# Filling the block-diagonal weights of the product by C with transfers, and pairing places 64 apart

## The chip, the cores and the metric

The kernel runs on one core of a Trainium2 chip. The metric is the device time of one execution in microseconds (us). The core's engines are called PE (TensorE; PEld is its weight loads), DVE (VectorE), ACT (ScalarE), POOL (GpSimd) and SP (SyncE, which issues nearly all transfers here). SBUF is the on-chip memory of 128 partitions, PSUM the memory that PE writes, DRAM the large memory outside the core.

## What is computed

The reference is a network of four layers. Each layer normalizes x (64 images of 11 x 11 = 121 positions, 128 channels), passes it through a state-space mixer and adds the result, then passes it through a feed-forward part that differs from layer to layer and adds that. The change lies in the mixer, which is the same in all four layers and takes most of the time. Its core, cut to what matters:

```
xs    = silu(conv1d(x @ in_proj))             # 256 places l, 121 channels d
Bs,Cs = projections of xs                     # 16 states n, two directions k
delta = softplus(projection of xs)
dA    = exp(delta * A)                        # per channel, state and place
dBu   = delta * Bs * xs
h     = scan over l of  h = dA * h + dBu
y     = einsum('bkdln,bknl->bkdl', h, Cs) + Ds * xs
y     = y[:, 0] + flip(y[:, 1])               # second direction runs backwards
```

The last product, y = sum over the 16 states n of h times C, is the one that is changed. For every image b, place l and channel d it is a sum of 16 terms whose weights C depend on b, n and l.

## The kernel before, in words

**Tiling.** A mixer handles the 64 images in eight chunks c of eight images (CB = 8). The 128 partitions hold the pairs (state n, image b), partition 8n + b. For each chunk there are two *passes* m = 2c and 2c + 1, one for each direction k (odd m goes backwards over the places). A pass runs over 61 pairs of channels, one *step* each; its first step is s = 61 m. A layer so has 16 passes and 976 steps, the kernel 64 passes.

**One step.** PE expands delta to the 128 partitions (`rows`, L677, into one of five PSUM tiles da; three steps ahead of the scan), ACT takes its exponentials (`exps`, L690), and DVE scans two channels (`scan`, L698) with da and the tile ub as inputs, into a tile H. ub holds delta times x for four channels, loaded from DRAM 14 steps ahead (`load_u`, L654, seven buffers, 512 KB each) and multiplied by B on POOL five steps ahead (`times_b`, L666). H and HX, two tiles, take the scans of 16 steps in turn (the groups dq = 0 to 3 of a pass).

**The product by C.** When a group of 16 steps is scanned, PE forms its y during the next 16 steps (`by_c`, L719): 32 *slots*, each four matmuls that lie beside each other in PE's columns. Each matmul takes 16 weights per partition: two places times eight images, where the weights are zero unless the partition's image is the column's. So one matmul sums over the 16 states for eight images, and two places share it. The results gather in the PSUM tile yb (eight slots); after every eight slots `keep_y` (L734 and L736) copies yb to the SBUF tile yst (even m, on ACT) or adds it there (odd m, on DVE). After each odd pass yst is stored to DRAM by 16 transfers (`store_y`, L751, 60.5 KB each) at steps 8 to 11 and 16 to 19 of the next pass.

**The weights.** `load_bc` (L636) loads B and C of a pass as two tiles Bt and Cp of 128 x 256, 18 steps before the pass. `own_c` (L643) makes the block-diagonal weights on POOL: a product of Cp, broadcast over eight columns, with a constant mask `own`, 128 x 512 elements, into one of four tiles Cz. It runs four times in a pass, at steps 8, 12, 16 and 20; slots 8u to 8u + 7 read Cz[u]. The group dq = 0 starts its product at step 16 of the pass.

**What sets the order.** The order is written out by hand: `run` puts each piece of work under a step (`self.at(step, f)`), and for every step the program issues, in this order, what is under `pre` (keep_y), the rows and exponentials of the step three ahead, loads and products of ub, the scan, and the plan of that step. Each engine takes its instructions in that order, SP's transfers too. Waits are set where data or buffers need them. A transfer on SP also takes one of eight semaphores in turn, so that an issue waits for the landing of the transfer eight before it.

In the even passes from m = 2 on, SP's queue holds, besides ub: the stores of y, the loads of R (L627, the operand of `rows`; the third part of a pass is loaded at step 20), and the loads ts and y of the tail of the chunk before (L453 and L455, at step 22), which PE and DVE use at steps 31 and 32.

Of the kernel before, what the change touches and what calls it, by code (L numbers as in the profile page):

```python
# [8 lines left out]
F32 = mybir.dt.float32  # L9
# [3 lines left out]
AX = mybir.AxisListType  # L13
# [3 lines left out]
D = 121  # L17
C = 128
L = 256
NS = 16  # L20
# [57 lines left out]
CB = 8  # L78
# [8 lines left out]
class Conv:  # L87
# [38 lines left out]
    def made(self, setup, fixed, ps, in_x, conv_wT, x_dt, dt_wT):  # L126
        cx, nc, a = self.cx, self.nc, self.cx.a
        p = f"L{self.l}_conv_"
        af = self.A.rearrange("p k d -> p (k d)")
        nc.scalar.activation(af, af, AF.Exp)  # L130
        nc.vector.tensor_scalar_mul(af, af, -1.0)


        pick = setup.tile([5 * 24, 5, CB], F32, name="pick")
        nc.vector.reduce_sum(pick, cx.ident[:120, :120].rearrange("p (a s b) -> p a b s", s=3, b=CB), axis=AX.X)
        self.pick = fixed.tile([5 * 24, 5, NS, CB], BF16, name="pick16")
        for i in range(5):
# [24 lines left out]

    def buffers(self, fixed, work, ps_f, dram):
        cx, nc, NC = self.cx, self.nc, self.NC
        self.work = work

        self.H = [fixed.tile([128, 2 * L, 16], F32, name="H"), cx.HX.rearrange("p (a w) -> p a w", w=16)]
        self.spare = [x.rearrange("p a w -> p (a w)") for x in self.H]
        self.da = [ps_f.tile([128, 2, L], F32, name=f"da{i}") for i in range(RING)]
        self.yb = ps_f.tile([128, 8, 2, 2, 16], F32, name="yb")  # L170
        nc.vector.memset(self.yb, 0.0)
        self.Cz = [fixed.tile([128, 64, CB], F32, name=f"Cz{i}") for i in range(4)]
        self.t = fixed.tile([128, CB, L], F32, name="t")
# [454 lines left out]
        if q == 3:  # L628
            nc.sync.dma_start(R[:24, 3, :], rows[24 * 120 : 24 * 121])

    def load_bc(self, m):
        c, k = m // 2, m % 2
        for name, at in (("Bt", 0), ("Cp", NS)):
            x = self.work.tile([128, L], F32, name=name, bufs=2)
            r0 = 2 * NS * k + at
            self.nc.sync.dma_start(x, self.bcD[c, r0 : r0 + NS].rearrange("r b l -> (r b) l"))  # L636
            self.bc[m, name] = x

    def own_c(self, m, u):

        C = self.bc[m, "Cp"]
        C = C[:, L - 1 - 64 * u : (L - 65 - 64 * u if u < 3 else None) : -1] if m % 2 else C[:, 64 * u : 64 * u + 64]
        self.nc.gpsimd.tensor_mul(  # L643
            self.Cz[u],
            C.unsqueeze(2).to_broadcast([128, 64, CB]),
            self.own.unsqueeze(1).to_broadcast([128, 64, CB]),
        )

    def load_u(self, T):
        m, i = divmod(T, TILES)  # L650
# [11 lines left out]
    def times_b(self, T):  # L662
        m, i = divmod(T, TILES)
        n = min(4, D - 4 * i)
        x = self.ub[T][:, :n, :]
        self.nc.gpsimd.tensor_mul(x, x, self.bc[m, "Bt"].unsqueeze(1).to_broadcast([128, n, L]))  # L666

    def channels(self, p):
        return min(2, D - 2 * p)
# [37 lines left out]
    def by_c(self, m, dq, slot):  # L707


        w = DQ[dq][1]  # L710
        H = self.H[dq % 2].rearrange("p (j l) w -> p l j w", l=L)
        for q in range(4):
            place = 8 * slot + 2 * q
            if m % 2:
                l = L - 1 - place
                h = H[:, l : (l - 2 if l > 1 else None) : -1, :, :w]
            else:
                h = H[:, place : place + 2, :, :w]
            self.nc.tensor.matmul(  # L719
                self.yb[32 * q : 32 * q + 16, slot % 8, :, :, :w],  # L720
                self.Cz[slot // 8][:, place % 64 : place % 64 + 2, :].rearrange("p l b -> p (l b)"),
                h,
                start=True,
                stop=True,
                skip_group_check=True,
            )
# [16 lines left out]
        if dq == 3:  # L743
            put(y[:, :, D - 1 : D], yb[:, :, 0, n : n + 1])

    def store_y(self, m, half, q, j):
        out = self.yD[m // 2].rearrange("(s x) (b d) -> x b s d", x=8, d=D)
        y = self.yst.rearrange("p (s x) d -> p s x d", x=2)
        rows = slice(16 * half, 16 * half + 16)
        p = 32 * q + 8 * j  # L750
        self.nc.sync.dma_start(out[2 * q + j][:, rows, :], y[p : p + 8, rows, j, :])  # L751


    def at(self, step, *fs):
# [15 lines left out]

    def run(self):
        NC, G = self.NC, 2 * self.NC * PAIRS
        self.R, self.bc, self.ub, self.pre = {}, {}, {}, {}
        NT = 2 * NC * TILES
        first = [PAIRS * (T // TILES) + 2 * (T % TILES) for T in range(NT)]

# [9 lines left out]
        for c in range(NC):  # L786
            s = STEPS * c
# [686 lines left out]
```

## Time and profile before

| what | value |
|---|---|
| median of 3 runs | 8470.6 us (8464.77 to 8479.49) |
| span of the profiled execution | 8458.2 us, 209204 instructions |
| PE busy | 5994.4 us (71%) |
| DVE busy | 6141.0 us (73%) |
| ACT busy | 5768.7 us (68%) |
| POOL busy | 5832.5 us (69%) |
| SP's transfers | 1588.21 MB, 930871 packets, 74.6% of the 16 transfer engines' time |
| mean granted clock of PE | 0.78 of full speed |
| mixers (first to last scan of each layer) | 79.5 to 1724.2, 2089.2 to 3728.0, 4037.8 to 5680.3 and 5994.4 to 7623.3 us |

The profile is of one execution. A line of a group of instructions reads: line of the kernel, engine, operation, written tile <- read tiles, shape, count | busy time in us, mean ns of one | idle time of the engine before it, and what ended most of that. In the view of waits a line reads: who waited <- for whom: us in all, times, the longest. In the timeline: start and length in us, engine, line, operation, tiles, how many; in square brackets the idle time before it and what ended that; SPq is SP issuing transfers, and its length there includes waits. A busy engine is not at its peak, and idle time of an engine that nobody waits for costs nothing.

### The profile page before, as it was taken

Reading aid. Unit: us, or ns where it says so; the run is one execution under the profiler, and the core shown is the slowest. Engines: PE = TensorE matmul, PEld = TensorE weight load, DVE = VectorE, ACT = ScalarE, POOL = GpSimd, SP = SyncE. Lnnn points to the kernel's source line nnn. Section 1 sums busy time; section 2 is a strip of 40 time slices with the busy share of each in tenths; the row PEclk is TensorE's granted clock in tenths of the full one; section 3 lists DMA queues with packets and bytes.
Section 4 is the critical chain, followed back from the end, with each engine's and each line's share of the span. In section 5 each row is a group of like instructions: output and inputs, shape, how many; then the busy total and the mean of one; then the engine's idle time right before and its main releaser. Section 6 shows DMA issues by size and latency. Waiting matters only on the chain.

```text
span 8458.2 us, 209204 instructions
## 1 busy us (share of the span) xinstructions
PE 5994.4 (71%) x83374; PEld 3445.8 (41%) x83374; DVE 6141.0 (73%) x8636; ACT 5768.7 (68%) x12927; POOL 5832.5 (69%) x3139
## 2 busy tenths in 40 slices
PE   5676677676677767767677777666567776766999
PEld 3343343355344434344344444344333433433445
DVE  6888888854888888872788888882688888883211
ACT  6888888743888878862788788863688888873210
POOL 6888888921988888850888888870688888890000
PEclk7777777767777777776777777766777778778999
DMA  6888998946898899960899999981689888992111
GB/s 171 221 224 223 223 226 225 232 140 177 218 224 225 224 220 222 230 181 25 222 220 227 221 226 226 224 205 31 179 226 225 230 225 226 226 231 72 39 34 37
DMA packets 933130, 1603.70 MB, mean 190 GB/s; under 512 B 139912, under 2 KB 620514, under 8 KB 932151
## 3 DMA queue, kind: packets, MB, share of 16 engines
q1 hardware_dynamic: 930871, 1588.21, 74.6%
q8 instruction: 655, 10.73, 0.6%
q14 instruction: 324, 2.65, 0.1%
q10 hardware_dynamic: 1280, 2.10, 0.1%
HBM read 1299.53 MB, written 290.52 MB: 188 GB/s over the span
## 4 chain that ended last, share of the span: by engine, by line
PE 31%; ACT 20%; DMA 17%; DVE 14%; issue 8%; POOL 7%; SPq 1%; DVEq 0%; POOLq 0%; ACTq 0%
ACT da L690 7%; DVE H L698 5%; DMA ub<-uD 5%; POOL ub L666 5%; PE da L677 4%; PE yb L719 4%; PE pc L253 4%; DVE HX L698 3%; DMA ts<-sD 3%; PE pu L1306 3%; PE acc L1309 3%; PE out L1349 2%; DMA uD<-u 2%; PE pst L1193 2%; DMA R<-dD 2%
## 5 line engine op out<-in xcount | busy, mean ns | idle before, releaser
L666 POOL TENSOR_TENSOR ub<-ub,Bt 128x1024 f32<-128x1024 f32 (+1 forms) x1984 | 4564.0, 2317 | 731.8 <-DMA ub<-uD 526.1
L690 ACT ACTIVATE da<-da,A 128x255 f32<-128x255 f32 x7744 | 3389.6, 446 | 1094.7 <-PE da L677 918.7
L698 DVE TENSOR_TENSOR_SCAN H<-da,ub 128x512 f32<-128x512 f32 x2048 | 2391.8, 1205 | 93.6 <-POOL ub L666 42.0
L677 PE MATMUL da<-R,pick 120*128 120x255 bf16 x7744 | 1783.5, 324 | 938.0 <-DVE H L698 529.4
L698 DVE TENSOR_TENSOR_SCAN HX<-da,ub 128x512 f32<-128x512 f32 (+1 forms) x1856 | 2115.6, 1187 | 90.5 <-issue 52.4
L677 PEld LDWEIGHTS <-pick 120*128 120x128 bf16 x7744 | 599.6, 104 | 1638.3 <-issue 777.1
L719 PE MATMUL yb<-H,Cz 128*16 128x64 f32 x32768 | 867.6, 255 | 349.8 <-ACT yst L736 260.4
L719 PE MATMUL yb<-HX,Cz 128*16 128x64 f32 x32768 | 856.5, 246 | 209.9 <-ACT yst L736 102.5
L719 PEld LDWEIGHTS yb<-H,Cz 128*16 128x16 f32 x32768 | 604.5, 112 | 921.4 <-issue 520.1
L719 PEld LDWEIGHTS yb<-HX,Cz 128*16 128x16 f32 x32768 | 562.4, 110 | 680.7 <-issue 316.8
L734 DVE TENSOR_TENSOR yst<-yst,yb 128x512 f32<-128x512 f32 (+2 forms) x640 | 340.2, 548 | 272.7 <-PE yb L719 272.5
L253 PE MATMUL pc<-w_conv,xnT 128*121 128x256 f32 x1344 | 441.6, 426 | 55.2 <-ACT t L257 55.1
L174 POOL MEMSET t<- 128x2048 f32 x4 | 7.2, 1804 | 597.4 <-PE px L1200 416.3
L736 ACT COPY yst<-yb 128x512 f32<-128x512 f32 (+2 forms) x640 | 330.6, 543 | 109.3 <-DMA yD<-yst 43.1
L304 PE MATMUL pd<-t,w_dt 122*128 122x512 f32 x480 | 358.3, 839 | 54.6 <-ACT t L264 54.6
L339 POOL TENSOR_TENSOR u<-relu,t 128x512 f32<-128x512 f32 x240 | 307.2, 1280 | 22.7 <-DVE relu L330 22.6
L350 POOL TENSOR_TENSOR d<-relu,d 128x512 bf16<-128x512 f32 x240 | 278.6, 1161 | 54.1 <-ACT d L346 53.9
L1273 DVE COPY U<-pu 128x488 f32<-128x488 f32 x128 | 85.4, 667 | 283.4 <-PE pu L1306 283.4
L1275 ACT COPY U<-pu 128x488 f32<-128x488 f32 x128 | 72.9, 569 | 309.2 <-PE pu L1306 309.2
L343 POOL TENSOR_TENSOR relu<-relu,d 128x512 f32<-128x512 f32 x240 | 279.1, 1163 | 6.6
L253 PEld LDWEIGHTS pc<-w_conv,xnT 128*121 128x121 f32 x1344 | 233.7, 209 | 102.8 <-ACT t L257 81.6
L643 POOL TENSOR_TENSOR Cz<-Cp,own 128x512 f32<-128x512 f32 x256 | 274.4, 1072 | 0.0
(242 smaller groups left out, 7929.8 us busy)
## 6 DMA issues: line engine op xcount, KB each, us to landing
ub<-uD SPq DMA_DIRECT2D x1920, 512.0 KB
dD<-d SPq DMA_DIRECT2D x256, 384.0 KB
R<-dD SPq DMA_DIRECT2D x192, 420.0 KB
uD<-u SPq DMA_DIRECT2D x256, 256.0 KB
sD<-s SPq DMA_DIRECT2D x128, 256.0 KB
yD<-yst SPq DMA_DIRECT2D x512, 60.5 KB
ts<-sD SPq DMA_DIRECT2D x56, 512.0 KB
y<-yD SPq DMA_DIRECT2D x112, 242.0 KB
```

Source lines behind the costliest of these rows:

```text
L253: nc.tensor.matmul(pc, lhs, rhs, start=(j == 0), stop=(j == taps - 1))
L304: nc.tensor.matmul(s["p"], self.w_dt[:, k, :], tb[: D + 1], start=True, stop=True)
L339: nc.gpsimd.tensor_mul(s["u"], s["relu"], tb)
L343: less.tensor_sub(s["relu"], s["relu"], s["d"][:, 0, :])
L350: less.tensor_sub(s["d"][:, 2, :], s["relu"], s["d"][:, 1, :])
L666: self.nc.gpsimd.tensor_mul(x, x, self.bc[m, "Bt"].unsqueeze(1).to_broadcast([128, n, L]))
L677: self.nc.tensor.matmul(self.da[g % RING][:, j, 1:], self.pick[:n, d % 5].rearrange("p n b -> p (n b)"), self.R[m, d // 35][:n, d % 35 // ...
L690: self.nc.scalar.activation(x, x, AF.Exp, scale=self.A[:, m % 2, d : d + 1])
L698: self.nc.vector.tensor_tensor_scan(self.H[dq % 2][:, :n, p - DQ[dq][0]], self.da[g % RING].rearrange("p j l -> p (j l)")[:, :n], x.rearra ...
L719: self.nc.tensor.matmul(self.yb[32 * q : 32 * q + 16, slot % 8, :, :, :w], self.Cz[slot // 8][:, place % 64 : place % 64 + 2, :].rearrange ...
L734: nc.vector.tensor_add(dst, dst, src)
L736: nc.scalar.copy(dst, src)
```

## The change

The tiles Cz become two, each laid out as two blocks x of 64 places by eight images, [128, x, b, 64], and both are cleared on POOL once per layer. `own_c`, its mask and the load of Cp go. Instead `load_c` fills, for each pass, each tile and each image b, the 16 partitions 8n + b of the image's own block from DRAM: 16 transfers per pass (two tiles, eight images), each of 16 x 2 x 64 elements, 8 KB. They stand at steps 9 and 10 (first tile) and 17 and 18 (second tile), four to a step. What lies outside an image's own block stays zero for the whole layer.

A matmul now takes the places l and l + 64 of one tile: its 16 weights stand 64 elements apart, and its moving rows are two places 64 apart. Slots 0 to 15 read the first tile, 16 to 31 the second. Since another place comes out where, `store_y` writes other rows of DRAM, in as many transfers of the same size.

```diff
-        self.own = fixed.tile([128, CB], F32, name="own")
-        nc.vector.reduce_sum(self.own, cx.ident.rearrange("p (n b) -> p b n", b=CB), axis=AX.X)
...
-        self.Cz = [fixed.tile([128, 64, CB], F32, name=f"Cz{i}") for i in range(4)]
+        self.Cz = [fixed.tile([128, 2, CB, 64], F32, name=f"Cz{i}") for i in range(2)]
+        for x in self.Cz:
+            nc.gpsimd.memset(x, 0.0)
...
-    def own_c(self, m, u):
-
-        C = self.bc[m, "Cp"]
-        C = C[:, L - 1 - 64 * u : (L - 65 - 64 * u if u < 3 else None) : -1] if m % 2 else C[:, 64 * u : 64 * u + 64]
-        self.nc.gpsimd.tensor_mul(
-            self.Cz[u],
-            C.unsqueeze(2).to_broadcast([128, 64, CB]),
-            self.own.unsqueeze(1).to_broadcast([128, 64, CB]),
-        )
+    def load_c(self, m, u, b):
+
+        rows = self.bcD[m // 2, 2 * NS * (m % 2) + NS : 2 * NS * (m % 2) + 2 * NS, b, :]
+        blocks = rows.rearrange("r (x l) -> r x l", l=64)
+        blocks = blocks[:, (1 - u) * 2 + 1 : (1 - u) * 2 - 1 if u == 0 else None : -1] if m % 2 else blocks[:, 2 * u : 2 * u + 2]
+        self.nc.sync.dma_start(self.Cz[u][b : b + 121 : CB, :, b], blocks)
...
+        C = self.Cz[slot // 16].rearrange("p x b l -> p (x b l)")
         for q in range(4):
-            place = 8 * slot + 2 * q
+            at = 4 * (slot % 16) + q
+            place = 128 * (slot // 16) + at
             if m % 2:
-                l = L - 1 - place
-                h = H[:, l : (l - 2 if l > 1 else None) : -1, :, :w]
+                l, at = L - 1 - place, 63 - at
+                h = H[:, l : (l - 65 if l > 64 else None) : -64, :, :w]
             else:
-                h = H[:, place : place + 2, :, :w]
+                h = H[:, place : place + 65 : 64, :, :w]
...
-                self.Cz[slot // 8][:, place % 64 : place % 64 + 2, :].rearrange("p l b -> p (l b)"),
+                C[:, at::64],
...
-    def store_y(self, m, half, q, j):
-        out = self.yD[m // 2].rearrange("(s x) (b d) -> x b s d", x=8, d=D)
+    def store_y(self, m, half, q, x):
+        out = self.yD[m // 2].rearrange("(h x s q) (b d) -> h x q b s d", h=2, x=2, q=4, d=D)
...
-            self.at(max(s - 18, 0), lambda m=m: self.load_bc(m))
-            for u in range(4):
-                self.at(s + 8 + 4 * u, lambda m=m, u=u: self.own_c(m, u))
+            self.at(max(s - 18, 0), lambda m=m: self.load_b(m))
+            for u in range(2):
+                for b in range(CB):
+                    self.at(s + 9 + 8 * u + b // 4, lambda m=m, u=u, b=b: self.load_c(m, u, b))
```

More of the change, by code (lines that the diff above doesn't have):

```diff
@@ L629, in load_r, with load_b @@
             nc.sync.dma_start(R[:24, 3, :], rows[24 * 120 : 24 * 121])
[L631 to L637, printed above, removed]
-    def own_c(self, m, u):
-        C = self.bc[m, "Cp"]
-        C = C[:, L - 1 - 64 * u : (L - 65 - 64 * u if u < 3 else None) : -1] if m % 2 else C[:, 64 * u : 64 * u + 64]
-        self.nc.gpsimd.tensor_mul(
-            self.Cz[u],
-            C.unsqueeze(2).to_broadcast([128, 64, CB]),
-            self.own.unsqueeze(1).to_broadcast([128, 64, CB]),
-        )
+    def load_b(self, m):
+        c, r0 = m // 2, 2 * NS * (m % 2)
+        x = self.work.tile([128, L], F32, name="Bt", bufs=2)
+        self.nc.sync.dma_start(x, self.bcD[c, r0 : r0 + NS].rearrange("r b l -> (r b) l"))
+        self.B[m] = x
+    def load_c(self, m, u, b):
[3 more added lines that the diff above has]
+        self.nc.sync.dma_start(self.Cz[u][b : b + 121 : CB, :, b], blocks)
     def load_u(self, T):
@@ L665, in times_b @@
         x = self.ub[T][:, :n, :]
-        self.nc.gpsimd.tensor_mul(x, x, self.bc[m, "Bt"].unsqueeze(1).to_broadcast([128, n, L]))
+        self.nc.gpsimd.tensor_mul(x, x, self.B[m].unsqueeze(1).to_broadcast([128, n, L]))
     def channels(self, p):
@@ L744, in keep_y @@
             put(y[:, :, D - 1 : D], yb[:, :, 0, n : n + 1])
-    def store_y(self, m, half, q, j):
-        out = self.yD[m // 2].rearrange("(s x) (b d) -> x b s d", x=8, d=D)
+    def store_y(self, m, half, q, x):
+        out = self.yD[m // 2].rearrange("(h x s q) (b d) -> h x q b s d", h=2, x=2, q=4, d=D)
         y = self.yst.rearrange("p (s x) d -> p s x d", x=2)
-        rows = slice(16 * half, 16 * half + 16)
-        p = 32 * q + 8 * j
-        self.nc.sync.dma_start(out[2 * q + j][:, rows, :], y[p : p + 8, rows, j, :])
+        self.nc.sync.dma_start(
+            out[half, x, q], y[32 * q + 8 * x : 32 * q + 8 * x + 8, 16 * half : 16 * half + 16, x, :]
+        )
     def at(self, step, *fs):
@@ L772, in run @@
         NC, G = self.NC, 2 * self.NC * PAIRS
-        self.R, self.bc, self.ub, self.pre = {}, {}, {}, {}
+        self.R, self.B, self.ub, self.pre = {}, {}, {}, {}
         NT = 2 * NC * TILES
```

## The prediction

> **What bounds the kernel now.** I read the page first, its busy times and its costliest groups, for what the change takes away:
>
> ```profile
> PE 5994.4 (71%) x83374; PEld 3445.8 (41%) x83374; DVE 6141.0 (73%) x8636; ACT 5768.7 (68%) x12927; POOL 5832.5 (69%) x3139
> ...
> L643 POOL TENSOR_TENSOR Cz<-Cp,own 128x512 f32<-128x512 f32 x256 | 274.4, 1072 | 0.0
> ```
>
> POOL (GpSimd) carries 5832.5 us, nearly as much as DVE, and L643, which goes, is 274.4 us of it: 256 products of 1.07 us, four in each of the 64 passes. Whether those are worth anything depends on who waits for POOL, so the view of waits is next:
>
> ```profile
> POOL ub L666 <- DMA ub<-uD: 526.1, 402, 13.4
> ...
> DVE yst L734 <- PE yb L719: 272.5, 175, 4.8
> ...
> DVE y L468 <- DMA y<-yD: 90.5, 23, 8.2
> ...
> DVE H L698 <- POOL ub L666: 42.0, 11, 12.8
> ...
> DVE HX L698 <- POOL ub L666: 9.5, 8, 3.1
> ```
>
> The reader is to see two things. POOL's longest wait is for a transfer, and the scans (L698), which pace a pass, wait for POOL only 42.0 + 9.5 us. DVE waits more for the product by C (PE, L719) and for loads. The view of the tile Cp shows the product once more, and below it (the line of PE's weight loads) who waited for it, us and times:
>
> ```profile
> L643 POOL TENSOR_TENSOR Cz<-Cp,own x256: 1055/1070/1122, 94.8 to 7570.7; 128x512 f32<-128x512 f32 x128
> ...
>   PEld yb L719: 38.7, 25
> ```
>
> So PE's weight loads waited 38.7 us for it in all.
>
> From the scans' starts in the trace (passes 2 to 14 of each layer) a pass of even m takes about 109 us and one of odd m about 99, and two scans of one unbroken run start 1.11 us apart. Even passes hold the loads of the next eight images, the tail of the last eight and, from m = 2 on, the 16 stores of y (L751), which stand in SP's queue among the loads of ub. The timeline of SP, and then of DVE, in one such pass (layer 0, m = 6; its step 17 ends at 740.7 us, its step 24 starts at 747.3 us):
>
> ```profile
> 741.03 0.51 SPq L654 DMA_DIRECT2D ub<-uD  x1
> 741.60 2.82 SPq L751 DMA_DIRECT2D yD<-yst  x4
> 744.55 0.64 SPq L654 DMA_DIRECT2D ub<-uD  x1
> 745.30 0.62 SPq L353 DMA_DIRECT2D dD<-d  x1
> 745.96 1.66 SPq L354 DMA_DIRECT2D uD<-u  x1
> 747.98 2.34 SPq L751 DMA_DIRECT2D yD<-yst  x4
> 750.42 0.65 SPq L654 DMA_DIRECT2D ub<-uD  x1
> ...
> 753.58 0.43 SPq L453 DMA_DIRECT2D ts<-sD  x1
> ```
>
> ```profile
> 738.66 15.91 DVE L698 TENSOR_TENSOR_SCAN HX<-da,ub 128x512 f32<-128x512 f32 x14
> ```
>
> From 741.60 to 750.42 SP issues 11 transfers in 8.82 us, 0.80 us each, without a pause: here **SP is full**, because the program gives SP's transfers eight semaphores in turn and an issue waits until the eighth one before it has landed. By the landing events in the trace a store of y takes 5.8 us from issue to landing (median; a tenth of them under 3.5), a load of ub 6.9. DVE meanwhile runs 14 scans without a gap, so nothing there can be late for free.
>
> **The change part by part.**
>
> *Removed on POOL.* 256 x 1.072 = 274 us. What it is worth is what others wait for: at most 42.0 + 9.5 + 38.7 = 90 us, at least nothing; I take 28, since most of those waits stand elsewhere in the passes. The 64 loads of Cp go too (SP, issued 18 steps ahead, 0.4 us each): 0.
>
> *Added on POOL and PE.* Two clearings per layer at its start; L174's row prices 128x2048 at 1804 ns, so an estimate of 0.9 us each, 7 us in all, beside 80 us before the first scan: 0. The first product on each new tile waits for up to seven semaphores; such a wait on PE's sequencer takes 51 ns by the trace, 128 x 6 x 51 ns = 39 us at most; it lies within the wait for the data: 0.
>
> *Moved on PE.* As many matmuls and weight loads, but the 16 weights of a partition lie 256 B apart and the moving rows in four runs of 64 B. Passes of odd m read such runs today (their places go backwards): their matmuls have 254 ns against 247 in even passes, so the runs cost nothing. No row has strided weights. Bounds: nothing, or as if all columns between were loaded, 209 ns (L253's load of 121 columns) instead of 97 to 112; nearest is the scan L698, which writes every sixteenth element and keeps its 1.11 us, so 0.
>
> *Stores of y.* As many, of the same size, other rows: 0.
>
> *Added on the transfer engines.* 4 x 16 x 16 = 1024 transfers of 32 pieces of 256 B. By the trace's packets a piece of 484 B takes 31 ns (median) and one of 1 KB 46: 32,768 x 31 ns / 16 = 63 us, less 64 x 128 x 46 ns / 16 = 24 us for Cp: +40 us of mean share over some 6,600 us, and the shares (0.86 to 0.93 in such stretches) have that room: 0.
>
> *Added in SP's queue, and on the path.* 16 more issues in each pass, at steps 9, 10, 17 and 18, behind a load of ub that waits for the scan of its own step. Behind them stand the next loads of ub, in even passes the stores of y, the load of R (step 20) and the tail's ts and y (step 22); and the product of slot 0 (slot 16) now waits for eight of them to land. By the trace, slot 0 starts 12.9 us after the end of scan 9 in even passes and 10.1 in odd ones; slot 16 starts 8.3 us after the end of scan 17 in even ones and 11.4 in odd ones. That is the time SP has.
>
> Even passes with stores (7 x 4 = 28): from the first store of the second burst, the last load of Cz1 is the 15th issue (4 stores, 4 loads, ub, 2 stores, 4 loads). At 0.7 us an issue (below the 0.80 above, as the new transfers are smaller) it goes out 14 x 0.7 = 9.8 us after 741.6 and lands 5 us later (between 3.5 and 5.8): 756.4, with 0.5 left over from the first burst 757. The product of slot 16 started at 749.9: it is 7 us late. PE takes its instructions in the program's order, so the rows of step 28 (L677) and their exponentials are late behind it, and DVE has at most a step in hand: **6 us per pass**, 168 us. The tail says the same: 16 x 0.7 = 11.2 us more for SP before ts and y, less 4.4 us that SP idles between the two bursts today, so they go out 6.8 us later; DVE waits for them now at step 32 (5.2 us per even pass). Both delays are one shift of the pass, so the larger is counted, not the sum.
>
> Odd passes (32): the loads of step 10 wait for the ub load of step 8 (8.2 us) eight places before; the last is issued some 9 us after scan 9 and lands at 11 to 13, against 10.1: 1 to 2.5 us late, of which PE and DVE have about one in hand: 1 us, 32 us. Their loads of ub have 10 us in hand there (4 on landing, 6 after POOL): 0. The 4 first passes, without stores: 2 us each, 8 us.
>
> Sum: 168 + 32 + 8 - 28 = **+180 us**. The profiled execution's span is 8458.2; the median of the runs is 8470.6, 12.4 more, which lies around the span and stays. 8470.6 + 180 = **8650 us**.
>
> Ends. Low: 0.45 us an issue and 3.5 to land puts slot 16 only 1.5 us late, 0.5 x 28 = 14, odd passes nothing, POOL worth 90: 8395. High: 0.84 us an issue (the mean of the second bursts) and 5.8 to land: 759.2, with 1.2 left over 10.5 late, 9.5 x 28 + 2.5 x 32 + 4 x 4 = 362: 8833.
>
> The Trainium skill ("DMA: Bandwidth & Descriptors", Rules for kernel authors) speaks against this change: many small transfers are to be made one, and under 64 KB one pays mostly overhead; these are 8 KB. Its Anatomy of one DMA puts the fixed part at about 2 us, where the trace has 5.8 us for stores of 60 KB behind full queues; with 2 us to land, slot 16 would be 4 us late and the sum an estimate of 8570. The measured landing decides.
>
> **The rivals.**
>
> *It is faster.* The small transfers go out at the fastest issue of a store, 0.35 us, and land in 3 us: 14 x 0.35 + 3 = 7.9 us, inside the 8.3 us that slot 16 leaves. Then nothing new is late and POOL's relief stands, up to 90 us: 8380 to 8450, say 8430. For it: SP is idle for two thirds of a pass. Against it: the 11 issues in 8.82 us. It decides at 8.3 us from scan 17 to the landing of Cz1.
>
> *Hidden anyway.* Half of the lateness is absorbed, and POOL's relief pays the rest: within 17 us of 8470.
>
> *Much slower.* SP's lag reaches the loads of R and ub in odd passes too (11 us per pass x 64 = 700), or strided weights load slowly: 8850 to 9200.
>
> **How the numbers follow.** The forecast's case (slower by 20 to 360 us) 0.60, faster 0.21, hidden 0.07, much slower 0.12. The range that takes in the ends is 8400 to 8830. About 0.2%, 17 us, is what a measurement of this kernel can tell from no change: faster 0.21, same 0.07, slower 0.72.
>
> **What would show it.** Right: in the view of waits, PE (yb, L715 then) waiting for transfers of Cz, mostly at step 24 of even passes; SP's timeline there without pauses, the tail's ts and y 5 to 8 us later after the first store; even passes 5 to 8 us longer, odd ones 0 to 2; POOL 274 us less busy and waiting longer for ub. Wrong: no such wait and shorter passes (faster), or weight loads over 112 ns (strided weights).

## The result and the profile after

The changed kernel takes 8891.2 us (median of 4 runs, 8871.1 to 8901.4); the kernel before took 8467.7 us in the runs beside it. The ratio is 1.050, with a 95% interval of 1.0481 to 1.0515: 423 us slower, where the forecast had 180 and a range that ended at 8830. The profiled execution's span is 8883.8 us against 8458.2. Below, "us slower" is always the difference of the medians of runs on one chip.

From the page of the changed kernel: the busy times, and the groups that answer to what the prediction priced (the product by B, and the scans into the tiles H and HX).

```profile
PE 6249.4 (70%) x83374; PEld 3701.2 (42%) x83374; DVE 6269.0 (71%) x8632; ACT 5876.7 (66%) x12927; POOL 5913.0 (67%) x2891
...
L660 POOL TENSOR_TENSOR ub<-ub,Bt 128x1024 f32<-128x1024 f32 (+1 forms) x1984 | 4836.1, 2466 | 1016.7 <-DMA ub<-uD 807.3
...
L692 DVE TENSOR_TENSOR_SCAN H<-da,ub 128x512 f32<-128x512 f32 x2048 | 2444.6, 1241 | 121.5 <-POOL ub L660 60.5
...
L692 DVE TENSOR_TENSOR_SCAN HX<-da,ub 128x512 f32<-128x512 f32 (+1 forms) x1856 | 2157.2, 1213 | 340.6 <-issue 233.8
```

POOL lost 256 products of 1.07 us, and is yet 80 us busier than before. The count of its instructions fell from 3139 to 2891; what rose is the mean of the product by B, from 2317 to 2466 ns (1984 of them: +296 us). The scans rose from 1205 and 1187 to 1241 and 1213 ns, in a line that the change does not touch. The same three groups on the page of the kernel before:

```profile
L666 POOL TENSOR_TENSOR ub<-ub,Bt 128x1024 f32<-128x1024 f32 (+1 forms) x1984 | 4564.0, 2317 | 731.8 <-DMA ub<-uD 526.1
...
L698 DVE TENSOR_TENSOR_SCAN H<-da,ub 128x512 f32<-128x512 f32 x2048 | 2391.8, 1205 | 93.6 <-POOL ub L666 42.0
...
L698 DVE TENSOR_TENSOR_SCAN HX<-da,ub 128x512 f32<-128x512 f32 (+1 forms) x1856 | 2115.6, 1187 | 90.5 <-issue 52.4
```

Something makes instructions longer on engines that do what they did before. It is not PE's granted clock, which is lower here (mean 0.764 for 0.778): in before_dummy below it is lower still, 0.758, and the three durations are 2316, 1207 and 1188 ns.

The view of waits of the changed kernel (who <- for whom: us in all, times, longest):

```profile
PE yb L715 <- DMA Cz<-bcD: 349.3, 66, 13.3
DVE yst L730 <- PE yb L715: 331.7, 210, 4.7
...
DVE y L467 <- DMA y<-yD: 59.7, 20, 6.3
```

The new wait stands there: PE's product by C waits 349.3 us for transfers into Cz, up to 13.3 us at a time. The scans' new gap (233.8 us on the page of the changed kernel, 52.4 before) is put down to "issue", which means that the view found no releaser; the timelines show which it is. First the view of the tile Cz, after and before (least, median and longest ns; then first and last start):

```profile
L715 PEld LDWEIGHTS yb<-H,Cz x32768: 104/146/196, 106.2 to 8045.0; 128*16 128x16 f32 x200
```

```profile
L719 PEld LDWEIGHTS yb<-H,Cz x32768: 92/97/151, 106.7 to 7619.8; 128*16 128x16 f32 x200
```

A weight load takes 146 ns at the median. Before it took 97.

Now the same even pass that the prediction showed (layer 0, m = 6), in the timeline of SP after the change, from the second half of the stores of y on. Step 17's scan ends at 773.2 us.

```profile
773.84 3.18 SPq L745 DMA_DIRECT2D yD<-yst  x4
777.12 6.30 SPq L641 DMA_DIRECT2D Cz<-bcD  x4
783.53 0.53 SPq L648 DMA_DIRECT2D ub<-uD  x1
784.15 0.55 SPq L352 DMA_DIRECT2D dD<-d  x1
784.76 0.62 SPq L353 DMA_DIRECT2D uD<-u  x1
785.42 2.08 SPq L745 DMA_DIRECT2D yD<-yst  x2
787.55 3.37 SPq L641 DMA_DIRECT2D Cz<-bcD  x4
790.97 0.84 SPq L745 DMA_DIRECT2D yD<-yst  x2
...
794.36 0.64 SPq L452 DMA_DIRECT2D ts<-sD  x1
```

The issue of the last transfer into the second tile, the 17th from the first store on, ends at 790.9, 17.1 us after that store began. Then PE's timeline over the same time:

```profile
792.38 0.87 PE L715 MATMUL yb<-H,Cz 128*16 128x64 f32 x24 [9.57 <-DMA Cz<-bcD]
793.18 0.61 PE L671 MATMUL da<-R,pick 120*128 120x255 bf16 x2
```

and DVE's:

```profile
770.85 11.51 DVE L692 TENSOR_TENSOR_SCAN HX<-da,ub 128x512 f32<-128x512 f32 x10
782.86 2.34 DVE L692 TENSOR_TENSOR_SCAN HX<-da,ub 128x512 f32<-128x512 f32 x2 [0.50 <-issue]
794.84 1.23 DVE L692 TENSOR_TENSOR_SCAN HX<-da,ub 128x512 f32<-128x512 f32 x1 [9.64 <-issue]
```

Read the three together: PE stands 9.57 us in front of slot 16; behind that product in PE's order are the rows of step 28 (L671, 793.18), then their exponentials on ACT, then the scan, which comes after 9.64 us without work. This chain is the one that the prediction described, and it is longer.

By the scans' starts (means of passes 2 to 14 of each layer), an even pass went from 107.4 to 117.5 us and an odd one from 99.5 to 103.6. Of the even ones' 10.1 us, 8.4 arise at the scan after step 27. The odd passes' 4.1 us are spread over many steps, none of which adds more than 0.9. So there are two losses of different shape: one gap in even passes, and something thin everywhere.

### The profile page after: what moved, and what is told of

It is laid out like the page before. It is cut to its first block, busy times and chain, and to the rows that moved or that the text cites. A ratio compares the mean times of both kernels' runs of the same rounds, so it can differ in the third digit from the quotient of the medians.

```text
span 8883.8 us, 210188 instructions
## 1 busy us (share of the span) xinstructions
PE 6249.4 (70%) x83374; PEld 3701.2 (42%) x83374; DVE 6269.0 (71%) x8632; ACT 5876.7 (66%) x12927; POOL 5913.0 (67%) x2891
## 4 chain that ended last, share of the span: by engine, by line
PE 31%; ACT 19%; DMA 18%; DVE 14%; issue 8%; POOL 6%; SPq 4%; DVEq 0%; POOLq 0%; ACTq 0%
DMA ub<-uD 8%; ACT da L684 6%; DVE H L692 6%; PE yb L715 5%; POOL ub L660 5%; PE da L671 4%; PE pc L252 3%; DMA ts<-sD 2%; PE pu L1303 2%; PE acc L1306 2%; DVE HX L692 2%; PE out L1346 2%; SPq L641 2%; PE pst L1190 2%; DMA bcD<-bc 2%
## 5 line engine op out<-in xcount | busy, mean ns | idle before, releaser
L660 POOL TENSOR_TENSOR ub<-ub,Bt 128x1024 f32<-128x1024 f32 (+1 forms) x1984 | 4836.1, 2466 | 1016.7 <-DMA ub<-uD 807.3
L692 DVE TENSOR_TENSOR_SCAN H<-da,ub 128x512 f32<-128x512 f32 x2048 | 2444.6, 1241 | 121.5 <-POOL ub L660 60.5
L671 PE MATMUL da<-R,pick 120*128 120x255 bf16 x7744 | 1795.5, 327 | 864.5 <-DVE H L692 509.3
L692 DVE TENSOR_TENSOR_SCAN HX<-da,ub 128x512 f32<-128x512 f32 (+1 forms) x1856 | 2157.2, 1213 | 340.6 <-issue 233.8
L715 PE MATMUL yb<-H,Cz 128*16 128x64 f32 x32768 | 956.6, 265 | 645.2 <-DMA Cz<-bcD 349.3
L671 PEld LDWEIGHTS <-pick 120*128 120x128 bf16 x7744 | 599.0, 105 | 1535.9 <-issue 748.2
L715 PEld LDWEIGHTS yb<-H,Cz 128*16 128x16 f32 x32768 | 706.3, 144 | 1243.6 <-issue 722.7
L715 PE MATMUL yb<-HX,Cz 128*16 128x64 f32 x32768 | 948.5, 256 | 187.1 <-ACT yst L732 91.9
L715 PEld LDWEIGHTS yb<-HX,Cz 128*16 128x16 f32 x32768 | 681.3, 146 | 651.7 <-issue 308.1
L349 POOL TENSOR_TENSOR d<-relu,d 128x512 bf16<-128x512 f32 x240 | 291.1, 1213 | 117.1 <-ACT d L345 114.8
L338 POOL TENSOR_TENSOR u<-relu,t 128x512 f32<-128x512 f32 x240 | 336.8, 1403 | 19.1 <-ACT da L684 18.5
L342 POOL TENSOR_TENSOR relu<-relu,d 128x512 f32<-128x512 f32 x240 | 303.0, 1262 | 8.2 <-ACT d L334 1.7
L374 PE MATMUL pb<-t,x_bc 121*64 121x512 f32 x256 | 179.1, 790 | 148.8 <-ACT bc L379 118.5
```

The costliest lines, as they stand in the source:

```text
L338: nc.gpsimd.tensor_mul(s["u"], s["relu"], tb)
L342: less.tensor_sub(s["relu"], s["relu"], s["d"][:, 0, :])
L349: less.tensor_sub(s["d"][:, 2, :], s["relu"], s["d"][:, 1, :])
L660: self.nc.gpsimd.tensor_mul(x, x, self.B[m].unsqueeze(1).to_broadcast([128, n, L]))
L671: self.nc.tensor.matmul(self.da[g % RING][:, j, 1:], self.pick[:n, d % 5].rearrange("p n b -> p (n b)"), self.R[m, d // 35][:n, d % 35 // ...
L692: self.nc.vector.tensor_tensor_scan(self.H[dq % 2][:, :n, p - DQ[dq][0]], self.da[g % RING].rearrange("p j l -> p (j l)")[:, :n], x.rearra ...
```

## The experiments

The theories. **The queue** (the prediction's): sixteen more places in SP's queue make the transfers late. **The weights' distance**: weights 256 B apart load slowly and hold up others; priced at nothing in the forecast. Rivals within these: the transfers cost by what they move, not by their number; the pairing of places 64 apart costs; PE's wait for Cz is the only way by which the queue reaches the scans.

### Parts of the change alone

**pool_paired**: the kernel before, with the pairing l, l + 64 and the new stores of y, but weights side by side and made on POOL.

```diff
-        self.Cz = [fixed.tile([128, 64, CB], F32, name=f"Cz{i}") for i in range(4)]
+        self.Cz = [fixed.tile([128, 32, 2, CB], F32, name=f"Cz{i}") for i in range(4)]
...
-                h = H[:, place : place + 2, :, :w]
+                h = H[:, place : place + 65 : 64, :, :w]
...
-                self.Cz[slot // 8][:, place % 64 : place % 64 + 2, :].rearrange("p l b -> p (l b)"),
+                self.Cz[slot // 8][:, at % 32].rearrange("p x b -> p (x b)"),
```

> The kernel before, with places l and l + 64 in one matmul: POOL still makes the weights (eight products of 128x256 elements in a pass instead of four of 128x512) and the 16 weights of a matmul still lie side by side. Only the moving rows lie 4 KB apart. Theory A (all of the 423 us are SP's queue and the wait for the weights' transfers): as before, 8468 us, or up to 30 more for the smaller POOL products. Theory B (weights 256 B apart slow the weight loads and the engines beside them): the same as A here, weight loads 110 ns, scans 1.20 us. Theory C (rows 4 KB apart do that): 100 to 200 us slower, scans 1.23 us or more.

Measured: ratio 1.0007 (0.9995 to 1.0018). Pairing and the other rows of the stores cost nothing.

**pool_strided**: the kernel before with its own places and POOL's products, only the 16 weights of a partition laid 256 B apart. No transfers.

```diff
-        self.Cz = [fixed.tile([128, 64, CB], F32, name=f"Cz{i}") for i in range(4)]
+        self.Cz = [fixed.tile([128, 2 * CB, 64], F32, name=f"Cz{i}") for i in range(2)]
...
-                self.Cz[slot // 8][:, place % 64 : place % 64 + 2, :].rearrange("p l b -> p (l b)"),
+                self.Cz[slot // 16][:, :, place % 128 // 2],
```

> The kernel before, with adjacent places in one matmul as before, made by POOL as before, but written so that the 16 weights of a matmul lie 256 B apart. No transfer is added. Theory A: as before, 8468 us, and weight loads of 110 ns. Theory B: weight loads of about 145 ns, POOL's products with B 2.45 us or more instead of 2.32, scans 1.21 to 1.24 us, and 100 to 200 us slower. Theory C: as before.

Measured: 1.0238 (1.0222 to 1.0254), 199 us slower. So the address step alone is slower by nearly half of what the whole change costs. The page of pool_strided:

```profile
L666 POOL TENSOR_TENSOR ub<-ub,Bt 128x1024 f32<-128x1024 f32 (+1 forms) x1984 | 4941.0, 2528 | 475.4 <-DMA ub<-uD 325.2
...
L698 DVE TENSOR_TENSOR_SCAN H<-da,ub 128x512 f32<-128x512 f32 x2048 | 2470.4, 1254 | 94.7 <-POOL ub L666 39.1
```

The reader is to see that the idle time of the scans stays as it was (94.7 us; 93.6 before) and the scans themselves are longer, 1254 for 1205 ns, more than the 1.24 us expected at most. This is no wait in the sense of the view of waits; only the mean duration tells of it.

**after_noload**: the changed kernel with the transfers into Cz made in the first pass of each layer only; all later passes use those weights, so this part of the product is changed.

```diff
-            for u in range(2):
+            for u in range(2 if m == 0 else 0):
```

> The changed kernel with the 16 transfers of C in the first pass of each layer alone; the other 15 passes use the first one's C, so that part of the product is left out. No POOL products, strided weights, hardly any transfers. Theory A: 8380 to 8470 us, since neither SP nor a wait is late and POOL has 274 us less. Theory B: 8500 to 8650 us, weight loads 145 ns and POOL's products with B still 2.45 us. The difference from the changed kernel, 8891, is what the transfers cost: by my count 240 to 400 us.

Measured: 1.0185 (1.017 to 1.02), 153 us slower. Without POOL's products and, but for a layer's first pass, without transfers, what is left is the distance of the weights.

**before_dummy**: the kernel before, with 16 transfers in each pass but a layer's last, from the same rows at the same steps, into a buffer of Cp that is overwritten before anything reads it. Nothing waits for them.

```diff
...
+            for u in range(2 if m + 1 < 2 * NC else 0):
+                for b in range(CB):
+                    self.at(s + 9 + 8 * u + b // 4, lambda m=m, u=u, b=b: self.spare_c(m, u, b))
```

> The kernel before, with the 16 transfers of C added at the same steps, but into a buffer of Cp that is not in use, which nobody reads (the real load comes later); not in the last pass of a layer. POOL makes the weights, and no matmul waits for a transfer. It has SP's crowded queue without the wait for the weights. If the queue alone (later ub, R, ts and y) is the cause: 150 to 250 us slower. If the wait of slot 16 is: 0 to 80 us slower, no gap of DVE at step 27 of even passes, and a longer one at step 32.

Measured: 1.0435 (1.0413 to 1.0456), 368 us slower. Transfers that no product waits for cost nearly as much as the whole change, and more than either case of the expectation allowed. The view of waits of before_dummy names the way, and beside it stands the same line of the kernel before:

```profile
ACT yst L746 <- DMA yD<-yst: 283.7, 33, 11.6
```

```profile
ACT yst L736 <- DMA yD<-yst: 43.1, 18, 4.1
```

In an even pass ACT copies the new product into yst (L746), which must not be before the stores of the old y have left it. Those stores stand in SP's queue among the new transfers. ACT takes its instructions in order, so the exponentials behind the copy are late, and the scan after step 29 with them (+6.9 us in even passes by the scans' starts). In the timelines of ACT and DVE in before_dummy (layer 0, m = 6) the copy and the scan come after gaps of 9.37 and 9.03 us:

```profile
791.60 0.65 ACT L746 COPY yst<-yb 128x512 f32<-128x512 f32 x1 [9.37 <-DMA yD<-yst]
```

```profile
793.15 2.34 DVE L708 TENSOR_TENSOR_SCAN HX<-da,ub 128x512 f32<-128x512 f32 x2 [9.03 <-issue]
```

The prediction did not have this wait.

**before_noown**: the kernel before with POOL's product into Cz in the first pass of each layer only; later passes use those weights (this part of the product is changed).

```diff
-            for u in range(4):
+            for u in range(4 if m == 0 else 0):
```

> The kernel before, with POOL's product of the weights in the first pass of each layer alone; the other 15 passes use the first one's weights, so that part of the product is left out. It measures what POOL's 274 us are worth. My prediction took 28 us and at most 90: 8380 to 8470 us against 8468. If POOL sets the pace: 150 to 270 us faster.

Measured: 0.9996 (0.9985 to 1.0006). POOL's busy time falls to 5594.2 us and the kernel is no faster: its waits for loads of ub grow from 526.1 to 696.1 us instead. The scans' wait for POOL's product by B stays too (39.0 us for 42.0 in its longer part). What the change was to save is worth 13 us at most by this interval, and nothing by its middle.

### What about the distance, what about the queue

**pool_pad65** and **pool_stride16**: pool_strided with weights 260 B and 16 B apart.

```diff
-        self.Cz = [fixed.tile([128, 2 * CB, 64], F32, name=f"Cz{i}") for i in range(2)]
+        self.Cz = [fixed.tile([128, 2 * CB, 65], F32, name=f"Cz{i}") for i in range(2)]
```

```diff
-        self.Cz = [fixed.tile([128, 2 * CB, 64], F32, name=f"Cz{i}") for i in range(2)]
+        self.Cz = [fixed.tile([128, 16, 2 * CB, 4], F32, name=f"Cz{i}") for i in range(2)]
...
-                self.Cz[slot // 16][:, :, place % 128 // 2],
+                self.Cz[slot // 16][:, place % 128 // 8, :, place % 8 // 2],
```

> The kernel with POOL's strided weights (pool_strided: 2.4% slower than before), but with the 16 weights of a matmul 260 B apart instead of 256. If only a step that is a power of two is slow: as before, 0 to 0.5% slower, weight loads of 110 ns, POOL's products with B 2.32 us. If each of 16 scattered reads costs: as pool_strided, 2.4% slower, weight loads of 145 ns and POOL's products with B 2.53 us.

> The same with the 16 weights 16 B apart, so that they lie within 256 B; POOL makes them in 16 small products per pass, not in four. If the distance costs: between before and pool_strided, weight loads of 110 to 130 ns. If any gap between weights costs: as pool_strided, weight loads of 145 ns, 2 to 3% slower (the small products on POOL may add up to 0.5%). If neighbours in one line of 64 B are one read, a quarter of pool_strided's loss.

Measured: 1.0026 (1.0016 to 1.0036) and 1.0023 (1.0013 to 1.0033). The weight loads of pool_strided and of pool_pad65, from the view of the tile Cz of each:

```profile
L719 PEld LDWEIGHTS yb<-H,Cz x32768: 104/146/199, 107.2 to 7805.3; 128*16 128x16 f32 x200
```

```profile
L719 PEld LDWEIGHTS yb<-H,Cz x32768: 104/109/152, 108.6 to 7651.8; 128*16 128x16 f32 x200
```

Weights that are scattered at these two steps cost 11 or 12 ns a load (108 and 109 for 97) and 0.2 to 0.3% of the kernel; weights at a distance of exactly 256 B cost 49 ns and 2.4%. Four bytes more in the step take nearly all of it away.

**dummy_two**: before_dummy with the same 512 pieces of 256 B in two transfers per pass instead of 16.

```diff
...
-                for b in range(CB):
-                    self.at(s + 9 + 8 * u + b // 4, lambda m=m, u=u, b=b: self.spare_c(m, u, b))
+                self.at(s + 9 + 8 * u, lambda m=m, u=u: self.spare_c(m, u))
```

> The kernel before_dummy (the 16 transfers of C into an unused buffer, 4.35% slower), with the same 512 pieces of 256 B in two transfers per pass, at steps 9 and 17, in place of 16. Theory of the issues (each takes a place in SP's queue and one of eight semaphores): 0 to 0.5% slower than before. Theory of the pieces (many small pieces keep the transfer engines busy): still about 4% slower.

Measured: 1.003 (1.0018 to 1.0042). The same pieces and bytes in two transfers cost 28 us; in 16 they cost 368. So it is the number of transfers that costs.

**dummy_first** and **dummy_second**: before_dummy with the burst of steps 9 and 10 only, and of steps 17 and 18 only (`range(1)` and `range(1, 2)` in its loop over u).

> before_dummy with only the first eight of its 16 spare transfers (steps 9 and 10); both bursts cost 1.0435. If the queue catches up between the bursts, as the forecast has it (SP idles some 4 us between them in the kernel before), this one costs little: 1.000 to 1.008. If the first burst's lateness is handed on to the second half of the stores, or if each burst costs alike, it is 1.015 to 1.025.

> before_dummy with only the last eight of its 16 spare transfers (steps 17 and 18), among the second half of the stores of y. If this burst alone makes the last stores late and they hold yst, it carries most of the cost: 1.025 to 1.04. If each burst costs alike, 1.015 to 1.025. If only both together exhaust what the queue has in hand, under 1.015.

Measured: 1.0116 (1.0101 to 1.0131) and 1.0229 (1.0214 to 1.0245). The first lies between its two cases, and the second does not carry nearly all. Together they cost 368 us, apart 93 and 190, in sum 283. The forecast had the queue catch up between the bursts; it does not.

### The changed kernel with one thing mended

**after_pad**: the changed kernel with the places 65 apart, so that the weights lie 260 B apart.

```diff
-        self.Cz = [fixed.tile([128, 2, CB, 64], F32, name=f"Cz{i}") for i in range(2)]
+        self.Cz = [fixed.tile([128, 2, CB, 65], F32, name=f"Cz{i}") for i in range(2)]
...
-                C[:, at::64],
+                C[:, at::65],
```

> After, with the places of Cz 65 apart instead of 64, so that the 16 weights of a partition lie 260 B apart; the transfers stay. If the cost of the distance of 256 B and the cost of SP's queue add up, some 200 us of the 423 go and the ratio to before is 1.025 to 1.03 (8690 to 8720 us), with weight loads at 97 ns again, scans at 1.21 us and the same waits for Cz and yst in even passes. If the two hide each other (the slower scans lie in time that the late transfers cost anyway), little goes: 1.035 to 1.05.

Measured: 1.034 (1.0319 to 1.0361), 279 us slower. Between the two cases: 144 us of the 423 went, where 200 were expected if the parts added up. That is near after_noload's 153 and not pool_strided's 199. In pool_strided POOL's products into Cz went on beside the slow loads; whether that makes the difference was not tried. The weight loads were expected at 97 ns and take 114 and 112. From the page of after_pad:

```profile
L660 POOL TENSOR_TENSOR ub<-ub,Bt 128x1024 f32<-128x1024 f32 (+1 forms) x1984 | 4575.4, 2322 | 1196.2 <-DMA ub<-uD 910.2
...
L692 DVE TENSOR_TENSOR_SCAN H<-da,ub 128x512 f32<-128x512 f32 x2048 | 2389.7, 1205 | 124.4 <-ACT da L684 62.3
...
L692 DVE TENSOR_TENSOR_SCAN HX<-da,ub 128x512 f32<-128x512 f32 (+1 forms) x1856 | 2128.6, 1189 | 358.9 <-issue 251.3
```

The durations are those of the kernel before (2317, 1205, 1187), and the idle times at least those of the changed kernel (1016.7, 121.5, 340.6): the two losses are taken apart. What is left, 279 us, is the cost of the transfers with weights 260 B apart, which alone cost 24 us in pool_pad65.

**after_dummy**: the changed kernel, weights 256 B apart, with the transfers of all passes but a layer's first into tiles that nothing reads. Its product uses the weights of the first pass of a layer (this part is changed).

```diff
+        self.Dz = [fixed.tile([128, 2, 64], F32, name=f"Dz{i}") for i in range(2)]
...
-        self.nc.sync.dma_start(self.Cz[u][b : b + 121 : CB, :, b], blocks)
+        dst = self.Cz[u][b : b + 121 : CB, :, b] if m == 0 else self.Dz[u][b : b + 121 : CB]
+        self.nc.sync.dma_start(dst, blocks)
```

> After, with the 16 transfers of each pass but the first of a layer written to tiles that nothing reads, so that no product waits for them; its product by C uses the weights of the first pass throughout (that part of the computation is changed). Weights 256 B apart without a wait for Cz stood at 1.0185. If PE's wait for Cz1 is what the transfers cost, it stands there again, 1.016 to 1.022. If the queue itself costs the time, by way of the late stores of y that hold yst and of the late loads behind them, it stays near after: 1.04 to 1.055.

Measured: 1.0514 (1.049 to 1.0538), as slow as the changed kernel. PE's wait for Cz is gone, and the time is not. Its view of waits:

```profile
PEld yb L717 <- ACT yst L734: 636.8, 233, 12.4
...
ACT yst L734 <- DMA yD<-yst: 273.9, 33, 10.8
```

The lateness comes by yst now. In the changed kernel's view no wait of ACT for yD stands at all: PE stops in front of slot 16 first, and while it stands, the stores leave; take that wait away and the copies into yst wait as long. Two waits hang on one late queue, and either alone is enough.

**after_pad_pool** and **after_pad_act**: after_pad with the 16 transfers issued on GpSimd, and on ACT. In the traces SP's and ACT's transfers take turns at the same eight semaphores (101 to 106, 108 and 109); GpSimd's have eight others (111 to 118).

```diff
-        self.nc.sync.dma_start(self.Cz[u][b : b + 121 : CB, :, b, :64], blocks)
+        self.nc.gpsimd.dma_start(self.Cz[u][b : b + 121 : CB, :, b, :64], blocks)
```

```diff
-        self.nc.sync.dma_start(self.Cz[u][b : b + 121 : CB, :, b, :64], blocks)
+        self.nc.scalar.dma_start(self.Cz[u][b : b + 121 : CB, :, b, :64], blocks)
```

> after_pad, with the 16 transfers issued on GpSimd instead of SP; GpSimd's transfers have eight semaphores of their own. If the places in SP's queue and its eight semaphores are the cost, most of what after_pad still loses goes: 0.998 to 1.01, with SP's lag and the wait of ACT for yst back near before, and GpSimd busier. If the transfers cost by what they move, or by landing late for slot 16 wherever they are issued, it stays at 1.02 to 1.03. GpSimd waits there for PE's last product on the tile, with the products by B queued behind it, which may cost some of it again.

> after_pad, with the 16 transfers issued on ACT instead of SP. They still take their turn at the same eight semaphores as SP's transfers. If SP's place in line alone is the cost, it stands near before: 0.998 to 1.01. If the eight shared semaphores are the cost, ACT itself now waits for landings of SP's loads, with exponentials queued behind: 1.03 or more.

Measured: 1.0079 (1.0056 to 1.0102) and 1.078 (1.0752 to 1.0807). Off SP, with semaphores of their own, the same transfers cost 55 us in all; an even pass takes 106.8 us, no longer than before, an odd one 101.2. So at least some 224 of the 279 us are the place in SP's queue and the wait for its semaphores. On ACT the transfers are dearer than on SP. The view of waits of after_pad_act:

```profile
ACT da L684 <- DMA Cz<-bcD: 167.5, 67, 5.1
...
ACT yst L732 <- DMA Cz<-bcD: 128.1, 28, 5.9
```

An exponential does not read Cz; it follows a transfer of Cz in ACT's order, and comes only when that has gone out. By the trace the 1024 issues take ACT 666 us (0.60 us each at the median), and ACT stands some 120 us more in front of them, mostly until a transfer of SP has landed. The first sum is paid on any engine that issues them (on GpSimd 514.5 us, where it hardly showed), so the shared semaphores are not shown to be the whole reason.

**after_pad_ypool** and its control **before_ypool**: after_pad and the kernel before, each with the stores of y issued on GpSimd.

```diff
-        self.nc.sync.dma_start(out[2 * q + j][:, rows, :], y[p : p + 8, rows, j, :])
+        self.nc.gpsimd.dma_start(out[2 * q + j][:, rows, :], y[p : p + 8, rows, j, :])
```

> after_pad with the 16 stores of y of an even pass issued on GpSimd, and the 16 transfers of C left on SP. In even passes SP then has as many issues as before the change. If the crowded queue is the cost, even passes come back to before and only the odd ones stay longer (2 us by after_pad, 32 passes): 1.000 to 1.015. If the transfers of C land too late for slot 16 by themselves, or wait for PE with the loads of ub behind them, it stays at 1.02 to 1.035.

> Before, with the 16 stores of y of an even pass issued on GpSimd instead of SP: the control for after_pad_ypool. ACT waits 43 us in all for the stores to free yst and DVE 90 us for y in the kernel before, so if the queue is already at its limit there, some of that goes: 0.988 to 0.998. If SP has just enough room, nothing: 0.998 to 1.002. If GpSimd's own issues and its wait for the copies of y hold the products by B: 1.002 to 1.015.

Measured: 1.0057 (1.0042 to 1.0072) and 1.0066 (1.0047 to 1.0085). Once the stores have left SP's queue, the kernel with the transfers of C on SP is no slower than the one without them. By passes, its even ones take 107.3 us (before_ypool 109.7, the kernel before 107.4) and its odd ones 102.2 (99.4 and 99.5): the crowd of the even passes is gone, as expected, and the small loss of the odd ones stays. In the kernel before, moving the stores does not pay: on GpSimd they cost 48 us. There the products by B queue behind them, and a wait of the scans for POOL's product rises from 9.5 us to this (view of waits of before_ypool):

```profile
DVE HX L698 <- POOL ub L666: 228.7, 103, 4.6
```

No version of the changed kernel that was run beats the kernel before.

## Why the prediction was right in direction and short in size

The forecast was +180: 168 for even passes, 32 for odd ones, 8 for first passes, less 28 for POOL. Measured +423. The missing 243 us are in three terms:

| term | forecast | measured | by |
|---|---|---|---|
| weights 256 B apart | 0 | 144 | 423 less after_pad's 279 |
| the transfers, on SP | 208 | 279 | after_pad (weights 260 B apart, relief 0) |
| relief of POOL | -28 | 0 | before_noown, -3 of 8470 |

Of the 279, 55 stay when GpSimd issues the same transfers, so at least some 224 are SP's queue.

- **Strided weights: the step that failed.** The prediction put the cost of weights 256 B apart at 0; it is 144 us. "Nearest is the scan L698, which writes every sixteenth element and keeps its 1.11 us, so 0." The row was of another engine that writes, not of PE that reads weights, and of a step of 64 B; the loads went from 97 to 146 ns. The bounds were nothing to 209 ns, so 146 lay within them, but the upper end was left out of the range: it stood as a rival, "strided weights load slowly", with 0.12 for itself and another mishap. Its own sign for this, weight loads over 112 ns, was met. And the price is not PE's own: its weight loads of the product by C are 221 us busier (604.5 + 562.4 to 706.3 + 681.3 on the two pages), beside matmuls. It is in what runs beside them: in pool_strided the scans are 161 us busier (2470.4 + 2198.4 for 2391.8 + 2115.6) and wait no longer. Sorted by the weight loads of the product by C that fall into it, a scan of the changed kernel takes 1215 ns with none and 1288 ns with 40 to 60 (in pool_strided 1220 and 1406); a product by B 2370 ns with none and 2835 ns with 60 to 80 (in pool_strided 2380 and 3011). In the kernel before both are nearly flat (1207 and 1197; 2362 and 2383), and in pool_pad65 too (1210 and 1203; 2364 and 2394). So POOL, which was to be 274 us less busy, is 80 us busier.
- **Even passes: mechanism right, size short.** Slot 16 was to be 7 us late; it starts 18.5 us after scan 17 for 8.3 before, so 10. The forecast counted 15 issues at 0.7 us, and 5 us to land. In 24 of the 28 even passes it is 17 issues (the stores of dD and uD, which the shown lines had, were not counted), in four it is 15; they take 16.0 us to the end of the last one, and 1.4 us more to the last landing (medians over the 28): 17.4 us in place of 14.8. Both sizes lie outside the forecast's bounds, on opposite sides: 0.94 us an issue (bounds 0.45 to 0.84), and 1.9 us from the start of the last issue to the last landing (bounds 3.5 to 5.8). The 2 us that the prediction took from the Trainium skill ("DMA: Bandwidth & Descriptors", Anatomy of one DMA) stand there for transfers issued on GpSimd; here, with transfers on SP, the 1.9 us are close to them. That the two errors make up for each other in part is luck. One us of the 10 was in hand, as the forecast had it; a part comes back at the tail's wait at step 32 (1.5 us less there; DVE's wait for y falls from 90.5 to 59.7 us). In after_pad an even pass is 7.8 us longer, where 6 were forecast: 28 x 1.8 = 50 us of the 71 by which the transfers were priced too low. (The prediction read an even pass of the kernel before as about 109 us; the mean is 107.4.)
- **What was missed there**: the buffer yst, by which the late stores reach ACT. In the changed kernel PE's wait comes first and covers it; after_dummy shows that it costs as much without that wait.
- **"With 0.5 left over from the first burst"**: dummy_first and dummy_second cost 93 and 190 us, both 368. We take it that each burst spends what the other had in hand; no run takes this apart.
- **Odd passes**: 1 us forecast, 2.0 in after_pad, 32 x 1 = 32 us more (with the 50, a little over the 71; first passes and the ends of layers were not taken apart). They keep 1.6 us with the transfers on GpSimd; where that comes from is open.
- **POOL's relief**: 28 taken of a bound of 90, measured nothing. With POOL's products gone, its wait for the loads of ub grew instead (526.1 to 696.1 us) and the scans' wait for POOL stayed, as POOL's longest wait in the profile could have said.
- **Costed at nothing and right**: the pairing (pool_paired), the bytes on the transfer engines (dummy_two, 28 us at most), the clearings (7.4 us).
- **Right**: the sign, the place (the second burst among the second half of the stores), PE's wait for Cz in the view of waits, the order PE, ACT, DVE in which it is handed on, and the tail's ts, which goes out 19.5 us after the first store for 12.0 before (medians), 7.5 us later where 5 to 8 were forecast. Even passes were to be 5 to 8 us longer and odd ones 0 to 2; both are outside that (10.1 and 4.1), and in after_pad both are just inside or at its edge (7.8 and 2.0). "Hidden anyway" and "faster" fall by that wait of 349.3 us. "Much slower" has the time, 8891, but not the way: strided weights do load slowly, yet alone they cost 144 to 199 us and not the 380 and more of its range, and the odd passes lose 4.1 us and not 11.

The Trainium skill ("DMA: Bandwidth & Descriptors", Rules for kernel authors), cited against the change, names the right fault: dummy_two moves the same bytes as before_dummy in an eighth of the transfers and costs 0.3% instead of 4.4%. The same page (Issuing engines are not separate DMA queues) has it that issuing from several engines saves only the time to initiate, which is usually small beside the transfer; here the time on SP, with the waits for semaphores in it, is most of the cost (1.034 on SP, 1.0079 on GpSimd), so the runs agree that there is something to save and not that it is small.

## What to carry to other kernels

Count the issues in a queue between two fixed points, all of them, and ask of every buffer that a late transfer holds, not only of the one that the change adds: here a wait taken away was replaced by the next one on the same queue. Where a layout puts weights 256 B apart, try one element of padding first; here it was worth 144 us of 8891, and the loss showed in the durations of the neighbours, not in any wait. And a busy engine whose own longest wait was for transfers gave nothing back here when work was taken from it.

## What the runs showed of the hardware

Weights 256 B apart load in 146 ns, 260 B apart in 109 to 114, 16 B apart in 108, side by side in 97 (medians of 16 columns). While such loads run, scans on VectorE and products on GpSimd, which use other tiles, take 6 and 20% longer where most of them fall in (15 and 27% in pool_strided); at 260 B they do not (scans no longer, products 1%, as in the kernel before). The Trainium skill ("SBUF — State Buffer", Who interferes with whom) has only the port pair that GpSimd and VectorE share as a cause of contention, and PE with ports of its own. The scans beside the 256 B loads (1288 for 1215 ns) show another; whether it lies in the memory's banks or in the read path was not tried, nor were other powers of two.
